# The start, the seam and the end of a two-layer block on one core: first loads in order of use, the last recurrence chunk in two, quarter stores

## The chip, the cores and the metric

The kernel runs on one core of a Trainium2 chip, which has eight. The metric is the device time of one execution in microseconds. TensorE (PE) multiplies, VectorE (DVE), ScalarE (ACT) and GpSimd (POOL) compute on tiles, and the sync engine's queue (SP) issues every DMA. All data is float32; each matmul therefore shows as two PE passes in the trace.

## The reference, cut to what matters

For x of shape (2, 4096, 256), with `ln` a layer norm without weights and `shift` a step by one position:

```
h = ln(x);  r, k, v = (h*mix_j + shift(h)*(1 - mix_j)) @ W_j.T          # j = r, k, v
wkv = scan over 4096 positions of (k, v) with a decay per channel, kept in log space
x1  = x + group_norm(sigmoid(r) * wkv) @ W_o.T      # statistics over all positions of a batch, per head
y   = ln(x1)
two layers:  y += local_attention(shift_token(y))    # 8 heads of 64, window 128, rotary
             y += gated_mlp(ln(shift_token(y)))      # 256 -> 2*682 -> 256, gelu
out = x1 + y
```

`shift_token` moves only the second half of the channels by one position. The group norm needs the whole sequence of a batch, so attention of a batch can't begin before its recurrence has ended.

## The kernel before

**Order.** The code does not issue instructions as it is written. `Plan` records every operation with its engine, its tiles and a row number (`plan.at`), and at the end `order` places them: each engine takes the operation that can start first by a table of costs, and among those the one with the lowest row and number. The result is one fixed queue per engine. In the trace nearly all instructions therefore have the line of `give` (L497, or L491 and L493 for `scaled`, which may go to DVE or ACT).

**Recurrence of batch 0.** `Recurrence(0, T, ...)` works through 4096 positions in eight chunks of T = 512. `ahead(c)` loads x, normalises it (`normed`), transposes it to xT (channels on partitions) and projects it to k, v, r. The mixing is folded into the weights: wnow is the weight times mix, wold the weight times (1 - mix), so each output takes four products (two halves of the channels, present and previous position). `scans(c)` does three scans on DVE for each half of the channels (m, the log sum, aa), exponentials and logarithms on ACT, and puts q to DRAM (zd) with its statistics; after the last chunk `group_norm` makes scale and offset (gmv, dm, group). Chunk c+1 is projected while chunk c is scanned. Part of this batch's tiles are lent from buffers that attention uses later (x, h, hm, hT, sq, t, qk); the rest lie in `arena`.

**Recurrence of batch 1** runs in chunks of TR = 256 beside the attention of batch 0, over the first 54 rows. It mixes x on DVE (`change`, `mix_x`) and uses the plain weights, which are loaded into wold again.

**Attention and MLP.** A row n is 128 positions of one layer and batch; a block k is four rows (512 positions). There are 128 rows and 32 blocks. A block's x is x plus the group-normed z times W_o (`mixed_out`, wot), or layer one's result from xmd. In each row there are the projection of the next row, scores, softmax, the values of the last row and the output projection (wo); `shift` copies x to h by DMA, h is normalised, and after four rows `transpose_h`, `gate`, `value` and `down` do the MLP (w, hm). `store` writes the block: to xmd for layer one; for layer two it loads x1, adds it on POOL and writes 512 KB to the output.

**Start.** SP loads mats, vec, mask, lnp, b1, qks, then wold (768 KB), then the first two chunks of x (512 KB each), then the weights of attention and MLP. The twelve scalings of the weights are the first large operations in DVE's queue:

```
for j in (1, 2, 0):
    for i in range(2):
        for dst, t in ((self.wnow, vec[:, j, i : i + 1]), (wold, omt[:, j, i : i + 1])):
            nc.vector.tensor_scalar(dst[:, j, i, :], wold[:, j, i, :], t, None, ALU.mult)
```

Of the kernel before, what the change touches and what calls it, by code (L numbers as in the profile page):

```python
# [15 lines left out]
P = 128  # L16
# [17 lines left out]
R_SLOTS = 54  # L34

FIRST = (
    ("xT", 2 * T + 2, 2),
    ("m ls aa", 2 * T + 2, 1),
    ("wnow", 6 * D, 1),
    ("k v r x f g e q", 2 * T, 2),  # L40
)
SECOND = (
    ("xT", 2 * TR + 2, 2),
    ("m ls aa", 2 * TR + 2, 1),
    ("x k v r", 2 * TR, 2),
    ("d f g e q", 2 * TR, 1),
    ("xm", 2 * TR, 3),
)
RA = 10764
VFIRST = True  # L50
# [122 lines left out]
class Plan:  # L173


    def __init__(self, nc, sbuf, psum, dram):
        self.nc, self.sbuf, self.psum, self.dram_pool = nc, sbuf, psum, dram
        for e in ("tensor", "vector", "scalar", "gpsimd", "sync", "either"):
            setattr(self, e, Engine(self, e))
        self.places, self.turns = {}, {}  # L180
        self.pieces, self.open, self.row = [], None, 0.0
        self.kept = 0
# [46 lines left out]
    def note(self, eng, name, args, kw):  # L229
# [35 lines left out]
        for v in ins:  # L265
            first = v.place.first
            if v.place.psum and first is not None and eng != "tensor":
                first.deps.update(d for d in before if d.n < first.n and d not in v.place.users)
# [232 lines left out]
def kernel(ctx: ExitStack, tc: tile.TileContext, a: dict, out: bass.AP):  # L501
# [12 lines left out]
    nc.sync.dma_start(out=mats, in_=a["c_mats"])  # L514
# [30 lines left out]
    nc.sync.dma_start(out=vec, in_=a["p_rwkv"])  # L545
    wot = tile_of([P, 2, D], "wot")

    wdec = tile_of([P, 2], "wdec")
    nc.scalar.activation(wdec, vec[:, 3, :], AF.Exp)
    nc.vector.tensor_scalar(wdec, wdec, -1.0, None, ALU.mult)  # L550

    mwu = tile_of([P, 2], "mwu")
    nc.vector.tensor_tensor(mwu, wdec, vec[:, 4, :], ALU.add)
    nc.vector.tensor_scalar(mwu, mwu, -0.5, None, ALU.mult)
# [5 lines left out]
    wold = tile_of([P, 3, 2, D], "wold")  # L560

    class Recurrence:


        def __init__(self, b, tr, spots, mixed):
            self.b, self.tr, self.mixed, self.spots = b, tr, mixed, spots
            self.turns = {}
            self.n = S // tr


            nc.sync.dma_start(out=wold, in_=a["w_rkv"])
            if not mixed:
                self.wnow = plan.view(*self.spot("wnow"), [P, 3, 2, D])
                omt = tile_of([P, 3, 2], "omt")
                nc.vector.tensor_scalar(omt, vec[:, 0:3, :], -1.0, 1.0, ALU.mult, ALU.add)
                for j in (1, 2, 0):
                    for i in range(2):
                        for dst, t in ((self.wnow, vec[:, j, i : i + 1]), (wold, omt[:, j, i : i + 1])):
                            nc.vector.tensor_scalar(dst[:, j, i, :], wold[:, j, i, :], t, None, ALU.mult)
            self.stats = tile_of([P, 2, S // 256, 6], "stats")[:, :, : self.n, :]  # L580

            self.m, self.ls, self.aa = (
                plan.view(*self.spot(t), [P, 2, tr + 1]) for t in ("m", "ls", "aa")
            )
            self.s0 = tile_of([P, 2], "s0")
# [3 lines left out]
            self.chunks = [{} for _ in range(self.n)]  # L589
# [6 lines left out]
        def t(self, tag, cols=None):  # L596
            return plan.view(*self.spot(tag), [P, 2, cols or self.tr])


        def load(self, c):  # L600
            x = self.chunks[c]["x"] = plan.view(*self.spot("x"), [P, self.tr // P, D])
            nc.sync.dma_start(
                out=x,
                in_=a["x"][self.b, c * self.tr : (c + 1) * self.tr, :].rearrange(
                    "(w p) d -> p w d", p=P
                ),
            )

        def normed(self, c):
            nw = self.tr // P  # L610
            x = self.chunks[c]["x"]
            mv = tile_of([P, NW, 2], "r_mv", 2)
            for w in range(nw):
                st = tile_of([P, 6], "r_st", 4)
                nc.vector.bn_stats(st, x[:, w, :])
                nc.vector.bn_aggr(mv[:, w, :], st)
            rs = tile_of([P, NW], "r_rs", 2)
            rsqrt_of(rs[:, :nw], mv[:, :nw, 1], nw, LN_EPS, ALU.add)
            nb = tile_of([P, NW], "r_nb", 2)
            nc.vector.scalar_tensor_tensor(  # L620
                nb[:, :nw], mv[:, :nw, 0], -1.0, rs[:, :nw], ALU.mult, ALU.mult
            )
            for w in range(nw):
                nc.scalar.activation(
                    x[:, w, :], x[:, w, :], AF.Identity, bias=nb[:, w : w + 1], scale=rs[:, w : w + 1]
                )

        def transposed(self, c):
            x, tr = self.chunks[c]["x"], self.tr
# [4 lines left out]
            else:  # L634
                nc.gpsimd.tensor_copy(xT[:, :, 0:1], self.chunks[c - 1]["xT"][:, :, tr : tr + 1])
# [10 lines left out]
        def change(self, c):  # L646
            ch = self.chunks[c]
            d = ch["d"] = self.t("d")
            nc.vector.tensor_tensor(d, ch["xT"][:, :, 1:], ch["xT"][:, :, : self.tr], ALU.subtract)

        def mix_x(self, c, j):
            ch = self.chunks[c]
            xm = ch["xm", j] = self.t("xm")
            for i in range(2):
# [4 lines left out]
                    ch["xT"][:, i, : self.tr],  # L659
                    ALU.mult,  # L660
                    ALU.add,
                )

        def project(self, c, j):

            ch, tr = self.chunks[c], self.tr
            if self.mixed:
                self.mix_x(c, j)
                parts = [(wold, ch["xm", j][:, i, :], i) for i in range(2)]
            else:  # L670
                parts = [
                    (wt, ch["xT"][:, i, off : off + tr], i)
                    for i in range(2)
                    for wt, off in ((self.wnow, 1), (wold, 0))
                ]
            dst = ch[j] = self.t("rkv"[j])
# [19 lines left out]
        def ahead(self, c):  # L696
# [3 lines left out]
            if self.mixed:  # L700
                self.change(c)
            for j in (1, 2, 0):
                self.project(c, j)


        def factors(self, y, c):

            g, e = self.t("g"), self.t("e")
# [6 lines left out]
        def scans(self, c):  # L715
            ch, tr = self.chunks[c], self.tr
# [3 lines left out]
            if c:  # L720
                nc.gpsimd.tensor_copy(m[:, :, 0:1], m[:, :, tr : tr + 1])
                nc.gpsimd.tensor_copy(ls[:, :, 0:1], ls[:, :, tr : tr + 1])
                nc.gpsimd.tensor_copy(aa[:, :, 0:1], aa[:, :, tr : tr + 1])
            f = self.t("f")
            for h in range(2):
                wd = wdec[:, h : h + 1]
                nc.vector.tensor_tensor_scan(
                    m[:, h, 1:], wd.to_broadcast([P, tr]), k[:, h, :], m[:, h, 0:1], ALU.add, ALU.max
# [10 lines left out]
            nc.scalar.activation(ls[:, :, 1:], e, AF.Ln)  # L739
# [7 lines left out]
            for h in range(2):  # L747
                nc.vector.tensor_tensor_scan(
                    aa[:, h, 1:], g[:, h, :], e[:, h, :], aa[:, h, 0:1], ALU.mult, ALU.add
                )  # L750
            q = self.t("q")
            for hs in hs2:
# [5 lines left out]
                for h in range(hs.start, hs.stop):  # L758
                    nc.vector.bn_stats(self.stats[:, h, c, :], q[:, h, :])
# [659 lines left out]
```

## Time and profile before

| | us |
|---|---|
| Median of 3 runs (range) | 3133.59 (3133.59 to 3134.77) |
| The profiled execution's own time | 3134.43 |
| Its span, first to last instruction | 3132.6 |
| PE / DVE / ACT / POOL busy | 3054.1 / 2528.4 / 1834.6 / 1323.1 |
| Mean granted clock of PE | 0.993 |
| DMA moved | 131.78 MB, 42 GB/s on average |

Busy time counts an engine as busy from an instruction's start to its end; the ends of matmuls are modelled. In a stage where PE is busy all the time, only less PE work could shorten it; where it stands idle, what it waits for sets the time. Times in the profile are microseconds from the first instruction.

### The profile page before, as it was taken

How to read it: one execution, taken by the hardware profiler on the slowest of the kernel's cores; microseconds unless marked ns; L12 is line 12 of the kernel's file. 1: busy time of each engine (PE TensorE's matmuls, PEld its weight loads, DVE VectorE, ACT ScalarE, POOL GpSimd, SP SyncE). 2: the span in 40 equal slices, each digit the busy share in tenths (PEclk: the TensorE clock that was granted, in tenths of full speed). 3: DMA queues.
4: the chain of work that ended last, by engine and by line, in shares of the span. 5: the costliest groups of instructions: out<-in, count | busy, mean ns of one | idle time of the engine just before them, and what ended most of it. 6: DMA issues, size and time to landing. Idle time of an engine off the chain costs nothing.

```text
span 3132.6 us, 47494 instructions
## 1 busy us (share of the span) xinstructions
PE 3054.1 (97%) x16296; PEld 2016.0 (64%) x16296; DVE 2528.4 (81%) x6287; ACT 1834.6 (59%) x4355; POOL 1323.1 (42%) x1544
## 2 busy tenths in 40 slices
PE   7969999999999999999999999999999999999998
PEld 3436666666666666666666666666666666666665
DVE  6979998888888988887778787777877877777774
ACT  5767766666666667655545555544555555555552
POOL 1217544445444444444444444444434443444431
PEclk9989999999999999999999999999999999999999
DMA  3122001111111111111112111111001111111000
GB/s 128 43 75 71 31 31 42 34 33 43 47 32 58 39 38 42 37 35 35 33 32 69 62 44 38 41 39 40 33 26 48 39 35 35 34 31 34 28 22 25
DMA packets 106386, 131.78 MB, mean 42 GB/s; under 512 B 11680, under 2 KB 89760, under 8 KB 105632
## 3 DMA queue, kind: packets, MB, share of 16 engines
q1 hardware_dynamic: 106144, 128.75, 13.1%
q8 instruction: 128, 2.10, 0.3%
q14 instruction: 114, 0.93, 0.1%
HBM read 78.38 MB, written 33.55 MB: 36 GB/s over the span
## 4 chain that ended last, share of the span: by engine, by line
PE 81%; DVE 9%; ACT 4%; issue 2%; DMA 1%; POOL 1%; SPq 0%; POOLq 0%; DVEq 0%; ACTq 0%
PE bank L497 81%; DVE arena L497 3%; DVE sq L497 1%; ACT arena L497 1%; DMA h<-x 1%; DVE qk L497 1%; ACT pr L497 1%; ACT L497 1%; DVE pr L497 1%; DVE pT L497 1%; DVE x L497 0%; DVE hm L497 0%; POOL rs L497 0%; ACT qk L497 0%; DVE pr L491 0%
## 5 line engine op out<-in xcount | busy, mean ns | idle before, releaser
L497 PE MATMUL bank<-wqkv,xT 128*128 128x512 f32 x1536 | 732.4, 600 | 0.0
L497 ACT ACTIVATE pr<-pr,nmx 128x256 f32<-128x256 f32 (+1 forms) x1024 | 504.6, 494 | 385.5 <-DVE nmx L497 385.3
L497 POOL TENSOR_TENSOR t<-qk,tab 128x256 f32<-128x256 f32 x512 | 385.9, 774 | 692.2 <-DVE qk L497 355.6
L497 PE MATMUL bank<-hT,w 128*128 128x512 f32 (+1 forms) x1408 | 645.7, 593 | 0.2 <-ACT hT L497 0.2
L497 PEld LDWEIGHTS bank<-hT,w 128*128 128x128 f32 (+1 forms) x1408 | 254.2, 189 | 254.6 <-issue 248.2
L497 PEld LDWEIGHTS bank<-wqkv,xT 128*128 128x128 f32 x1536 | 264.2, 190 | 228.4 <-issue 226.1
L497 DVE CUSTOM_DVE_ANT_0 pr<-bank,mask 128x256 f32<-128x256 f32 (+1 forms) x1024 | 373.3, 414 | 40.2 <-PE bank L497 40.0
L497 POOL TENSOR_TENSOR rn<-rn,mhalf 128x16 f32<-128x16 f32 x128 | 376.9, 2945 | 10.4
L497 PE MATMUL bank<-w,hm 128*128 128x256 f32 x1536 | 352.4, 379 | 1.8 <-DVE hm L497 1.8
L497 PEld LDWEIGHTS bank<-w,hm 128*128 128x128 f32 x1536 | 288.9, 190 | 59.8 <-issue 21.5
L497 PEld LDWEIGHTS bank<-mats,pr 128*128 128x128 f32 x2016 | 237.1, 141 | 117.0 <-issue 76.3
L493 ACT ACTIVATE pr<-pr,sums 128x256 f32<-128x256 f32 (+1 forms) x615 | 285.9, 496 | 44.1 <-DVE sums L497 43.0
L497 PEld LDWEIGHTS bank<-pT,vt 128*64 128x64 f32 x4032 | 217.5, 137 | 93.8 <-issue 85.4
L497 PE MATMUL bank<-mats,pr 128*128 128x128 f32 x2016 | 270.7, 273 | 6.3 <-DVE pr L491 4.3
L497 PE MATMUL bank<-kT,qT 64*128 64x256 f32 (+1 forms) x2048 | 253.7, 386 | 3.3 <-DVE nmx L497 3.3
L497 PE MATMUL bank<-pT,vt 128*64 128x128 f32 x4032 | 248.4, 276 | 0.0
L497 PE MATMUL bank<-wo,oT 128*128 128x256 f32 x1024 | 244.8, 382 | 0.7 <-ACT oT L497 0.7
L497 POOL TENSOR_TENSOR tab<-tab,qks 128x256 f32<-128x256 f32 x128 | 164.5, 1286 | 187.6 <-DMA tab<-in_c_rot_dram 159.3
L497 PEld LDWEIGHTS bank<-wo,oT 128*128 128x128 f32 x1024 | 192.2, 190 | 76.9 <-issue 36.4
L497 ACT COPY pT<-bank 128x512 f32<-128x512 f32 (+1 forms) x280 | 153.0, 573 | 123.9 <-PE bank L497 123.0
L497 DVE TENSOR_TENSOR x<-x,bank 128x256 f32<-128x256 f32 (+1 forms) x288 | 128.0, 445 | 119.5 <-PE bank L497 115.5
L497 PEld LDWEIGHTS bank<-kT,qT 64*128 64x128 f32 x2048 | 184.8, 186 | 44.2 <-issue 20.7
(140 smaller groups left out, 4893.8 us busy)
## 6 DMA issues: line engine op xcount, KB each, us to landing
tab<-in_c_rot_dram SPq DMA_DIRECT2D x128, 128.0 KB
x<-in_x_dram SPq DMA_DIRECT2D x20, 512.0 KB
z<-zd SPq DMA_DIRECT2D x16, 512.0 KB
x1d<-x SPq DMA_DIRECT2D x16, 512.0 KB
x<-x1d SPq DMA_DIRECT2D x16, 512.0 KB
h<-x SPq DMA_DIRECT2D x128, 64.0 KB
xmd<-x SPq DMA_DIRECT2D x16, 512.0 KB
x<-xmd SPq DMA_DIRECT2D x16, 512.0 KB
```

Of the source, the lines that this page charges most:

```text
L493: self.nc.scalar.activation(dst, src, AF.Copy, scale=scale)
L497: getattr(getattr(self.nc, o.eng), name)(*args, **kw)
```

## The change

- **Loads.** Batch 0's first chunk of x comes first, in four pieces of 128 positions; then mats, vec and wold in three parts (k, v, r). `normed` works on two pieces at a time. wot, mask, lnp, b1 and qks are loaded after the first chunk's scans (`plan.hold` makes a load wait for an operation), the weights of attention and MLP after those of chunks 1 to 3.
- **Weight scaling** goes to DVE or ACT, in the order k, v, r, and is placed behind the first chunk's normalisation.
- **The last chunk** of batch 0 is two chunks of 256. Batch 1's first chunk is projected behind it with the scaled weights (`split`); only then is wold loaded again and the rest of batch 1 mixed on DVE (`mixed`).
- **Other places.** `ahead` puts load, normalisation and transposition one row earlier; z is scaled on ACT instead of POOL; `transpose_qk` is recorded earlier in its row; the first row of the next block's h is copied at the end of the block before it.
- **x1** is loaded at a layer-two block's first `shift`, and added on POOL row by row two rows later, before `down` adds the MLP. `store` is gone: `down` stores each quarter of a block (128 KB).
- **early**: in the last block an MLP value's bank need not wait for the other inputs of the operation that reads it.

The diff, cut to its core:

```diff
+AHEAD = 1
-            if v.place.psum and first is not None and eng != "tensor":
-                first.deps.update(d for d in before if d.n < first.n and d not in v.place.users)
+            if v.place.psum and first is not None and eng != "tensor" and not self.early:
+                first.deps.update(d for d in before if d.n < first.n)
+        if self.hold is not None:
+            before.add(self.hold)
...
         def load(self, c):
+            nw = self.len[c] // P
+            x = self.chunks[c]["x"] = plan.view(*self.spot("x"), [P, nw, D])
+            step = 1 if c == 0 else nw
+            for w in range(0, nw, step):
+                o = self.off[c] + w * P
+                nc.sync.dma_start(
+                    out=x[:, w : w + step, :],
+                    in_=a["x"][self.b, o : o + step * P, :].rearrange("(w p) d -> p w d", p=P),
+                )
...
+        def mixed(self, c, j):
+            ch, tr = self.chunks[c], self.len[c]
+            if "d" not in ch:
+                d = ch["d"] = self.t("d", tr)
+                nc.vector.tensor_tensor(d, ch["xT"][:, :, 1:], ch["xT"][:, :, :tr], ALU.subtract)
+            xm = self.t("xm", tr)
+            for i in range(2):
+                nc.vector.scalar_tensor_tensor(
+                    xm[:, i, :], ch["d"][:, i, :], vec[:, j, i : i + 1],
+                    ch["xT"][:, i, :tr], ALU.mult, ALU.add,
+                )
+            return [(wraw, xm[:, i, :], i) for i in range(2)]
+
+        def split(self, c, j):
+            ch, tr = self.chunks[c], self.len[c]
+            return [
+                (wt, ch["xT"][:, i, off : off + tr], i)
+                for i in range(2)
+                for wt, off in ((wnow, 1), (wold, 0))
+            ]
...
+        def ahead(self, c, how):
+            row = plan.row
+            plan.at(row - 1)
             self.load(c)
             self.normed(c)
             self.transposed(c)
+            plan.at(row)
             for j in (1, 2, 0):
+                self.project(c, j, how)
...
         for h in range(2):
-            nc.gpsimd.tensor_scalar(
-                z[:, h, :], z[:, h, :], g[:, 0, h : h + 1], g[:, 1, h : h + 1], ALU.mult, ALU.add
+            nc.scalar.activation(
+                z[:, h, :], z[:, h, :], AF.Identity, bias=g[:, 1, h : h + 1], scale=g[:, 0, h : h + 1]
             )
...
+        elif c < NB - 1:
+            hs[k + 1] = tile_of([P, NW, D], "h", 2)
+            nc.sync.dma_start(out=hs[k + 1][0:1, 0, P:], in_=x[P - 1 : P, w, P:])
         nc.sync.dma_start(out=h[:, w, :P], in_=x[:, w, :P])
+        if l:
+            if w == 0:
+                x1s[k] = tile_of([P, NW, D], "x1")
+                nc.sync.dma_start(out=x1s[k], in_=x1d[b][c])
+            row = plan.row
+            plan.at(row + 2)
+            nc.gpsimd.tensor_tensor(x[:, w, :], x[:, w, :], x1s[k][:, w, :], ALU.add)
+            plan.at(row)
...
         nc.vector.tensor_tensor(x, x, py, ALU.add)
-
-    def store(k):
         l, b, c = blocks[k]
-        x = xs.pop(k)
-        if l == 0:
-            nc.sync.dma_start(out=xmd[b][c], in_=x)
-            return
-        x1 = tile_of([P, NW, D], "x1")
-        nc.sync.dma_start(out=x1, in_=x1d[b][c])
-        nc.gpsimd.tensor_tensor(x, x, x1, ALU.add)
-        nc.sync.dma_start(
-            out=out[b, c * T : (c + 1) * T, :].rearrange("(w p) d -> p w d", p=P), in_=x
-        )
+        o = c * T + w * P
+        to = out[b, o : o + P, :] if l else xmd[b][c][:, w, :]
+        nc.sync.dma_start(out=to, in_=x)
...
-    rec = Recurrence(0, T, spots(FIRST, lent), False)
-    rec.ahead(0)
+    plan.at(-101)
+    rec = Recurrence(0, [T] * (NB - 1) + [T // 2] * 2, T, spots[0])
+    rec.start()
+    rec.load(0)
+    nc.sync.dma_start(out=mats, in_=a["c_mats"])
+    nc.sync.dma_start(out=vec, in_=a["p_rwkv"])
+    for j in (1, 2, 0):
+        nc.sync.dma_start(out=wold[:, j], in_=a["w_rkv"][:, j])
+    rec.normed(0)
+    small_vectors()
+
+    for j in (1, 2, 0):
+        for i in range(2):
+            for dst, t in ((wnow, vec[:, j, i : i + 1]), (wold, omt[:, j, i : i + 1])):
+                nc.either.scaled(dst[:, j, i, :], wold[:, j, i, :], t)
+    rec.transposed(0)
+    for j in (1, 2, 0):
+        rec.project(0, j, rec.split)
+    rec2 = Recurrence(1, [TR] * (S // TR), TR, spots[1])
     for c in range(rec.n):
         if c + 1 < rec.n:
             plan.at(-90 + c)
-            rec.ahead(c + 1)
-        if c == 0:
-            nc.sync.dma_start(out=wot, in_=a["w_ot"])
-        if c == 1:
-            weights(0, "qkvo12")
+            rec.ahead(c + 1, rec.split)
         plan.at(-90 + c)
         rec.scans(c)
+        plan.hold = plan.pieces[-1][0]
+        if c == 0:
+            later_loads()
+        if 0 < c < 4:
+            weights(0, ("qkv", "o", "12")[c - 1])
+        plan.hold = None
     rec.group_norm()
+    for c in range(AHEAD):
+        plan.at(-0.5)
+        rec2.ahead(c, rec2.split)
+    plan.at(-0.5)
+    nc.sync.dma_start(out=wraw, in_=a["w_rkv"])
+    rec2.start()
```

## The prediction

> **What bounds the kernel now.** I read the page's first two parts, then busy time by stage, then the order of time where TensorE (PE) is not busy.
>
> ```profile
> PE 3054.1 (97%) x16296; PEld 2016.0 (64%) x16296; DVE 2528.4 (81%) x6287; ACT 1834.6 (59%) x4355; POOL 1323.1 (42%) x1544
> ```
>
> PE bounds: 3132.6 - 3054.1 = 78.5 us is all it stands still. The busy time by stage (start:end, length, PE, PEld, DVE, ACT, POOL, granted clock, DMA share, GB/s) says where:
>
> ```profile
> 0.00:20.00 20.00, 2.23 (x7) 1.35 (x8) 7.67 (x34) 3.56 (x6) 3.19 (x16) 1.00 0.86 295
> ...
> 40.00:200.00 160.00, 154.36 (x398) 70.08 (x396) 140.31 (x223) 122.36 (x208) 37.41 (x51) 1.00 0.14 50
> 200.00:240.00 40.00, 18.46 (x69) 15.04 (x70) 29.57 (x75) 15.82 (x26) 11.57 (x24) 0.66 0.34 112
> 240.00:360.00 120.00, 106.54 (x610) 73.06 (x609) 109.46 (x289) 84.76 (x203) 80.53 (x99) 0.96 0.17 55
> 360.00:600.00 240.00, 236.90 (x1278) 156.95 (x1277) 214.38 (x534) 164.07 (x379) 103.12 (x130) 1.00 0.09 29
> 600.00:1500.00 900.00, 894.70 (x4948) 608.18 (x4947) 778.94 (x1934) 569.98 (x1350) 405.98 (x461) 1.00 0.13 40
> 1500.00:3080.00 1580.00, 1580.00 (x8792) 1056.18 (x8792) 1224.37 (x3166) 855.59 (x2161) 675.08 (x757) 1.00 0.12 38
> ```
>
> Idle: 17.8 at the start, 5.6 in the first recurrence, 21.5 between recurrence and attention (there the clock is 0.66 too), 13.5 while attention fills, 3.1 and 5.3 until 1500, none to 3080, 11.7 at the end. From 1500 on a change can only cost. The places, in order of time (start, length, engine, instruction, idle before it):
>
> ```profile
> 10.48 0.62 DVE L497 TENSOR_SCALAR arena<-wold,vec 128x256 f32<-128x256 f32 x2 [6.64 <-DMA wold<-in_w_rkv_dram]
> ...
> 17.72 2.80 PE L497 MATMUL bank<-mats,hm 128*128 128x128 f32 x8 [17.72 <-ACT hm L497]
> ...
> 20.46 1.95 PE L497 MATMUL bank<-arena 128*128 128x512 f32 x2
> ...
> 219.36 0.59 PE L497 MATMUL bank<-gmv,mats 128*128 128x2 f32 x2 [20.01 <-DVE gmv L497]
> ...
> 231.25 1.02 PE L497 MATMUL bank<-wot,z 128*128 128x256 f32 x4
> ...
> 3126.29 2.34 POOL L497 TENSOR_TENSOR x<-x,x 128x1024 f32<-128x1024 f32 x1 [33.02 <-DVE x L497]
> 3128.65 0.39 SPq L497 DMA_DIRECT2D out_dram<-x  x1
> ```
>
> The normalisation of the first x stands on VectorE (DVE) behind twelve weight scalings that wait for one 768 KB load. In the middle PE has run out of projections at 199.35 and waits for the last chunk's scans to give the group statistics (gmv). At the end a POOL addition stands between the last matmul and the store.
>
> **Part A, the start: -9.9.** After the change SP issues four 128 KB pieces of x first, then mats, vec and wold in three pieces, at 0.4 to 0.5 us each. Before, vec was issued at 1.17 and had landed at 3.04 (1.9 us), and 1.37 MB had landed by 10.48, about 175 GB/s once it flowed. So x pieces land at about 3.3 to 5, mats and vec before 6, wold's k third near 7.5. Statistics of two pieces to nb: 0.4 + 0.16 on DVE and 1.1 on POOL, as at 219.50 to 220.83 before. ScalarE (ACT) then has two x pieces (0.52 each), wdec, one weight scaling that waits for wold's k, and the last two x pieces: done near 9.3. Transposes and two copies of 0.6: projection runs from 11.0. Before, 48 passes of 0.43 ended at 41.56, so it effectively ran from 20.9. Bounds: 8 if the k third lands at 9.5, 11.5 if loads flow at the 405 GB/s seen between 10 and 20 us. The clock is taken as full, as the first row shows (1.00 while PE idles).
>
> **Part B, the middle: -6.4 more, to the first wot matmul.** Everything up to the last recurrence chunk shifts by A: PE needs 22.5 us a chunk, DVE some 19.7, both nearly full, so no more than the shift. The last 512 columns become two chunks of 256 with the same columns in all (48 matmuls of 256 for 24 of 512), ending near 189.4. Behind them the other batch's first chunk is projected with 24 matmuls of 256 where 12 did (wnow and wold instead of mixed x): 12 x 2 x 0.215 = +5.2 us of PE work, put where PE idled; six mixing operations of 0.42 and a subtraction go from DVE (-3.1). PE is through at about 200.5.
>
> Then DVE decides. Counting the changed order from the first half chunk's m scan to gmv, with start-to-start times of before: 14 scans of 256 columns x 0.66, 2 of 512 x 1.2, 7 operations of 256 x 0.42, 25 of 512 elements x 0.60, 14 statistics x 0.31, 11 tiny ones 1.1: 34.9 us. That includes the other batch's normalisation, copies and mixing, which are ahead of gmv in DVE's queue. It starts where chunk 7's scan stood, 183.28 - 9.9 = 173.4; with 4 us of waits (6.6 before) gmv comes near 212, not 219.36. A rule speaks against the halves: each chunk needs ACT's table changed to Ln and back, two changes more. The row:
>
> ```profile
> 201.90 1.28 ACT L497 ACT_TABLE_LOAD   x1 [1.40 <-DVE qk L497]
> 203.19 1.06 ACT L497 ACTIVATE arena<-qk 128x1024 f32<-128x1024 f32 x1
> ```
>
> It costs 1.28, and Ln starts 1.29 after it. The Trainium skill ("ScalarE: Activation LUTs", What ACT_TABLE_LOAD costs) charges a drain of about 1.38 besides, 2.66 in all. By the row the two cost 2.6, part of it under the other half's DVE work, and are inside my 4 us; by the page 5.3, and gmv would come near 214.5. I take the row.
>
> From gmv to the first wot matmul: before 11.9, behind 16 projection passes at half clock; after, 1.4 to dm, 4.8 to group as before, then z on ACT (2 x 0.55) instead of POOL: 7.4, so 219.4. The reload of wold is issued only when the last half chunk frees x buffers (near 208) behind two 512 KB loads of x; 1.79 MB at about 260 GB/s (the rate between 200 and 204 before): landed near 216, and the 8 passes ahead of wot hide it. So wot comes 11.9 us earlier, with 8 projection matmuls (3.4) and 8 transposes (1.1) more already done: 16.3 in all, A included.
>
> Clock: before, it was 0.50 from 204 to 230:
>
> ```profile
> 204.00:219.00 15.00, 0.00 (x0) 0.00 (x0) 12.03 (x21) 7.13 (x12) 0.00 (x0) 0.50 0.32 107
> 219.00:230.00 11.00, 8.46 (x24) 6.30 (x25) 8.98 (x33) 3.28 (x6) 7.05 (x12) 0.50 0.22 72
> ```
>
> The skill ("TensorE: Matmul & The Clock Gate", Part 1) has it halve after one idle window of about 3.4 us. By it a remaining gap of 11 us goes cold again, so I give nothing back for the clock; only a gap under 3.4 would save about 4 more. The same rule makes idle the cold default, which the start's 1.00 contradicts; by it A would shrink only if the warm-up cost differed between the two kernels.
>
> **Part C, attention's beginning (240 to 600): -3.** DVE is 91% busy there. It loses 3.1 of mixing, POOL loses 32 z operations (25.9 us), ACT gains 32 x 0.59 at 70% busy. In the only long stall PE held h transposes for a normalised h for 4.3 us; the changed order has all eight of the block after the next row's wo, about half a row later. What other stalls the new order makes the trace cannot say: from -8 to +6, and I take -3, near DVE's saving.
>
> **Part D, the end: -0.9.** x1 is added four times per block by POOL two rows ahead, so after the last DVE addition (3126.20) a 128 KB store follows. Before: 2.43 to the issue, 3.95 to the span's end with 512 KB. With 128 KB I estimate 2.8: -3.5 in all (bounds -2.4 with equal landing, -4). Against it: before, the last wo was followed by 12 down passes (2.6 us) which hid part of the wait for the last h; in the changed order these come ahead of wo and PE goes straight to h: +2.6. The early flag gives nothing, since PE runs without a gap from 3094.97 to 3125.7.
>
> **Nothing for the rest.** Stores in quarters are 96 issues more of 0.4 us on SP, which has four or five a row of 21.3 us; later loads and the moved 0.5 KB row of h likewise; x1's load waits on POOL's last addition to the one buffer, with h copies queued behind it on SP. The cover is the distance from h to its transposes: shift at 2668.24, h transposed at 2688.89, some 10 us after it is ready. Without this cover each of 16 blocks would cost its lateness. I keep -1 to +4.
>
> **Sum.** -16.3 - 3 - 0.9 = -20.2 against the profiled execution's 3134.43 gives 3114.2. That execution lies 0.84 above the median of 3133.59, inside its spread of 1.2; I predict 3114.
>
> **The rivals.** (1) Only the start moves: half chunks meet the same chain DVE-ACT-table, ACT with two more tables and the other batch's four normalisations is late, gmv near 217, or attention's beginning eats the lead: 3121 to 3126. For it: DVE and ACT both near full before gmv. Against: half-chunk work interleaves. Chance 0.15. (2) The gap nearly closes: waits vanish, gmv by 206, PE stays warm: 6 + 4 more, 3101 to 3107. Chance 0.15. (3) Slower: SP's queue. In 16 layer-two blocks the x1 load waits for POOL's last addition and holds the next row's h copies; the price is the lateness beyond the 10 us of cover, and it decides from 1.3 us per block (16 x 1.3 = 21), so an x1 load 11 us late. POOL is 42% busy, which speaks against. 3136 to 3150, chance 0.03. (4) The lead is real but waited away: 3127 to 3140, 0.04. Forecast 0.63, its own range 3107 to 3121.
>
> Range 3102 to 3126: bounds of A (+-1.8), gmv (+-4), C (-5, +9), D (+-1). What a measurement can tell from no change is about 0.2%, 6.3 us; below 3127.3 is faster: 0.93, same 0.04, slower 0.03.
>
> **What would show it.** First transposes near 8 and projection from 11; gmv near 212 with PE idle 10 us before it, clock 0.5 again; wot near 219; last h stall of about 7 us; span end 3 us after the last DVE addition; 1500 to 3080 still full. Projection from later than 14, gmv after 217, or PE gaps between 600 and 3080 make it wrong.

## The result, and the profile after

The changed kernel takes 3111.93 us (median of 6 runs, 3107.07 to 3113.52) where the kernel before takes 3134.47 beside it (3133.59 to 3136.11): a ratio of 0.9926, 95% interval 0.9913 to 0.9939, or 22.5 us. The prediction was 3114.0, range 3102 to 3126. The profiled execution took 3112.78, in the upper half of its runs, with a span of 3110.8.

The page's busy time of the changed kernel:

```profile
PE 3061.6 (98%) x16368; PEld 2030.8 (65%) x16368; DVE 2539.1 (82%) x6306; ACT 1865.0 (60%) x4401; POOL 1339.6 (43%) x1581
```

PE now stands still for 3110.8 - 3061.6 = 49.2 us instead of 78.5, and works 7.5 us more, of which 5.2 are the twelve additional matmuls of 256. So 29.3 us of idle time went. Busy time by stage says where (start:end, length, PE, PEld, DVE, ACT, POOL, clock, DMA share, GB/s):

```profile
0.00:20.00 20.00, 12.52 (x26) 5.79 (x27) 9.42 (x31) 7.04 (x14) 4.70 (x20) 1.00 0.47 145
...
40.00:200.00 160.00, 148.98 (x427) 77.23 (x425) 135.84 (x245) 124.93 (x211) 45.66 (x67) 0.99 0.22 76
200.00:240.00 40.00, 32.09 (x118) 25.63 (x119) 31.82 (x75) 24.41 (x40) 11.26 (x22) 0.76 0.40 132
240.00:360.00 120.00, 118.58 (x695) 79.91 (x694) 114.31 (x323) 93.53 (x228) 84.78 (x101) 1.00 0.16 51
360.00:600.00 240.00, 238.09 (x1301) 161.27 (x1300) 216.55 (x543) 165.77 (x385) 108.45 (x133) 1.00 0.12 37
600.00:1500.00 900.00, 892.86 (x4925) 603.06 (x4924) 774.11 (x1904) 581.42 (x1362) 403.34 (x462) 1.00 0.13 39
```

At the start, 7.5 us idle in the first 20 instead of 17.8. Between 40 and 240, 18.9 instead of 27.2: the one gap of 20 us is broken up, not closed. Between 240 and 360, 1.4 instead of 13.5: here the most was won. Between 600 and 1500, 7.1 instead of 5.3: a small loss. PE in order of time (idle before it in brackets):

```profile
10.17 2.08 PE L497 MATMUL bank<-arena 128*128 128x512 f32 x2
12.04 1.91 PE L497 MATMUL bank<-arena,wold 128*128 128x512 f32 x2
...
35.60 1.13 PE L497 MATMUL bank<-arena 128*128 128x512 f32 x2 [1.59 <-DVE arena L497]
...
200.15 1.40 PE L497 MATMUL bank<-mats,arena 128*128 128x128 f32 x4 [6.51 <-ACT arena L497]
...
218.58 0.38 PE L497 MATMUL bank<-gmv,mats 128*128 128x2 f32 x2 [3.63 <-DVE gmv L497]
...
227.19 6.50 PE L497 MATMUL bank<-wot,z 128*128 128x256 f32 x16 [2.21 <-ACT z L497]
...
3075.40 1.33 PE L497 MATMUL bank<-mats,h 128*128 128x128 f32 x5 [7.51 <-DVE h L497]
```

gmv comes at 218.58, only 0.8 before its old place (219.36), and wot at 227.19 instead of 231.25. The 6.5 us at 200 are new. ACT in order of time shows what they wait for:

```profile
190.82 1.28 ACT L497 ACT_TABLE_LOAD   x1
...
193.80 1.28 ACT L497 ACT_TABLE_LOAD   x1
...
199.50 2.06 ACT L497 ACTIVATE arena<-arena,r_nb,r_rs 128x256 f32<-128x256 f32 x4
```

The other batch's first chunk is normalised (199.50) behind two table loads and the exponentials of a half chunk. At the end the last store follows DVE's last addition directly:

```profile
3107.67 0.42 DVE L497 TENSOR_TENSOR x<-x,bank 128x256 f32<-128x256 f32 x1 [2.17 <-PE bank L497]
3108.12 0.33 SPq L497 DMA_DIRECT2D out_dram<-x  x1
```

Two marks serve below: the start of row 0's scores and of row 5's. Idle time of PE up to the first, between the two, and the half-clock windows up to 600 in the trace's clock records, which begin with the first change to full clock:

| kernel | idle to row 0 | idle rows 0 to 5 | half clock | median |
|---|---|---|---|---|
| before | 46.9 | 11.5 | 37.5 | 3134.5 |
| changed | 28.4 | 0.0 | 23.9 | 3111.9 |
| 1: last chunk whole | 28.5 | 8.8 | 27.3 | 3121.6 |
| 2: first chunk not ahead | 38.4 | 1.0 | 23.9 | 3113.9 |
| 3: z on POOL | 33.7 | 8.4 | 37.5 | 3131.7 |
| 5: before, z on ACT | 45.7 | 9.6 | 34.1 | 3127.8 |
| 9: whole old start | 38.8 | 0.0 | 27.3 | 3123.4 |

Five parts of the change were undone, each by itself, in the changed kernel, and a few things were added. The earlier place of `transpose_qk`, the early copy of h's first row, `early` and the quarter stores of layer one alone were not undone singly. The kernel before, run beside them, had medians of 3134.3 to 3135.2. One caution: run 8 has the changed kernel's order up to the last row, and yet its profile is 3 us ahead from row 0 on, with 20.5 us of half clock instead of 23.9. Both wait 2.04 us for the second half chunk's transposed x, the changed kernel at 181.34 and run 8 at 180.62; behind it the changed kernel has half clock from 181.65 to 185.06, and run 8 has none. Differences of 3 us between two profiles' early parts are therefore no finding by themselves.

### The profile page after: what moved, and what is told of

The parts are those of the page before. It is cut to its first block, busy times and chain, and to the rows that moved or that the text cites. A ratio compares the mean times of both kernels' runs of the same rounds, so it can differ in the third digit from the quotient of the medians.

```text
span 3110.8 us, 47943 instructions
## 1 busy us (share of the span) xinstructions
PE 3061.6 (98%) x16368; PEld 2030.8 (65%) x16368; DVE 2539.1 (82%) x6306; ACT 1865.0 (60%) x4401; POOL 1339.6 (43%) x1581
## 3 DMA queue, kind: packets, MB, share of 16 engines
q1 hardware_dynamic: 114592, 128.75, 13.2%
## 4 chain that ended last, share of the span: by engine, by line
PE 80%; DVE 10%; ACT 4%; POOL 2%; issue 2%; DMA 2%; SPq 0%; POOLq 0%; DVEq 0%; ACTq 0%
PE bank L497 80%; DVE arena L497 3%; ACT arena L497 1%; DMA h<-x 1%; DVE pr L497 1%; DVE sq L497 1%; DVE qk L497 1%; POOL rs L497 1%; ACT L497 1%; DVE hm L497 1%; POOL rn L497 1%; DVE x L497 1%; ACT qk L497 0%; SPq L497 0%; DVE pT L497 0%
## 5 line engine op out<-in xcount | busy, mean ns | idle before, releaser
L497 POOL TENSOR_TENSOR rn<-rn,mhalf 128x16 f32<-128x16 f32 x128 | 380.9, 2976 | 10.3
L497 PEld LDWEIGHTS bank<-kT,qT 64*128 64x128 f32 x2048 | 184.9, 186 | 44.6 <-issue 19.8
L497 POOL TENSOR_SCALAR rs<-mv 128x1 f32<-128x1 f32 x192 | 98.4, 517 | 248.4 <-DVE mv L497 242.2
L497 PE MATMUL bank<-arena,wold 128*128 128x256 f32 (+1 forms) x600 | 193.1, 447 | 0.0
```

The source lines that it names most:

```text
L497: getattr(getattr(self.nc, o.eng), name)(*args, **kw)
```

## The experiments

**1. The last chunk whole.**

```diff
-    rec = Recurrence(0, [T] * (NB - 1) + [T // 2] * 2, T, spots[0])
+    rec = Recurrence(0, [T] * NB, T, spots[0])
```

> Changed kernel with the last recurrence chunk of batch 0 whole (512 columns) again; the rest stays, the other batch's first chunk behind it too. Theory (the halves cost more than they bring: two more table changes and a ping-pong between ACT and DVE; the start alone would have brought gmv to about 219.4 - 8.5 = 211): gmv near 213 to 216 instead of 218.6, time 2 to 5 us below the changed kernel (3107 to 3110). Rival (the halves shorten the last chain, as the prediction had it): gmv near 222, time 3 to 6 us above it (3115 to 3118).

3121.63 us (3120.78 to 3122.18), ratio 0.9958 (0.9943 to 0.9973): 9.7 above. Both theories missed. PE in order of time:

```profile
211.08 0.58 PE L497 MATMUL bank<-gmv,mats 128*128 128x2 f32 x2 [9.62 <-DVE gmv L497]
...
218.01 5.37 PE L497 MATMUL bank<-wot,z 128*128 128x256 f32 x16 [4.11 <-ACT z L497]
```

gmv is 7.5 us earlier without the halves and wot 9.2, as my theory said, and still the kernel is slower. What PE waited for between row 0 and row 5 (total, times, longest), and the busy time there:

```profile
PE bank L497 <- DVE h L497: 4.2, 1, 4.2
PE bank L497 <- DVE pr L491: 1.7, 1, 1.7
PE bank L497 <- DVE qk L497: 1.5, 1, 1.5
```

```profile
251.50:339.70 88.20, 79.38 (x497) 56.22 (x496) 80.94 (x217) 64.73 (x165) 53.82 (x63) 0.94 0.14 46
```

The same stretch of the changed kernel:

```profile
262.10:333.90 71.80, 71.80 (x481) 51.86 (x480) 69.11 (x202) 54.93 (x152) 57.15 (x61) 1.00 0.15 49
```

With the whole chunk attention begins 10.6 us earlier, but with 10.7 us less matmul work done ahead, and DVE has 80.9 us to do in five rows instead of 69.1. PE waits for it 8.8 us, and partly at half clock. Up to row 0 both idle alike (28.5 and 28.4). The halves pay in rows 0 to 5, not at gmv: at row 5 this kernel is 5.8 us behind. Another 3.5 us come after row 5, and their cause is open.

**2. The other batch's first chunk in row 0, mixed.**

```diff
-AHEAD = 1
+AHEAD = 0
...
+                if c == 0:
+                    rec2.ahead(0, rec2.mixed)
```

> Changed kernel with the other batch's first chunk in row 0 again (mixed x, 12 matmuls of 256 instead of 24), not ahead of attention. Theory (the projection ahead fills only what the gap had free; the lead in attention's beginning comes with it): PE work 5.2 us less, gap in front of gmv about 8 us longer but gmv 2 to 4 us earlier, stalls between 240 and 360 back by 3 to 6 us: 1 to 5 us above the changed kernel. Rival (stalls in attention's beginning have another cause, z on POOL or order): idle time between 240 and 360 stays near 1.4 us, time 3 us below the changed kernel to equal.

3113.87 us (3112.85 to 3115.74), ratio 0.9934 (0.9919 to 0.9949): 1.9 above, inside both intervals. Ten more us idle up to row 0, gmv at 213.65, 4.9 earlier, 11.1 us less matmul time spent when row 5 is reached, at the same time (333.9 in both). Only 5.2 us of it are the additional matmuls; the rest isn't made up later either (PE is busy for 3050.4 us in all, where the changed kernel has 3061.6), as the changed kernel projects partly at half clock. The theory holds in size and in gmv's direction, though only 1 us of the stalls came back. The additional matmuls were paid for by the gap, and little more.

**3. z on POOL again.**

```diff
-            nc.scalar.activation(
-                z[:, h, :], z[:, h, :], AF.Identity, bias=g[:, 1, h : h + 1], scale=g[:, 0, h : h + 1]
-            )
+            nc.gpsimd.tensor_scalar(
+                z[:, h, :], z[:, h, :], g[:, 0, h : h + 1], g[:, 1, h : h + 1], ALU.mult, ALU.add
+            )
```

> Changed kernel with z scaled on POOL again instead of ACT. Theory (z on ACT is a small part: first wot about 1.5 us earlier, the rest is the lead): 1 to 3 us above the changed kernel, idle time between 240 and 360 below 5 us. Rival (POOL's 32 z operations of 0.8 us held up h and so made the stalls of attention's beginning): idle time between 240 and 360 back at 8 to 13 us, time 6 to 12 us above.

3131.73 us (median of 20, 3130.0 to 3134.47), ratio 0.9992 (0.9985 to 0.9999): 19.8 above, nearly the kernel before. The theory fell, the rival is right and still too small. Busy time of the stage:

```profile
240.00:360.00 120.00, 108.12 (x595) 73.58 (x594) 101.92 (x279) 78.19 (x187) 82.54 (x101) 0.93 0.16 52
```

11.9 us idle instead of 1.4. POOL in order of time:

```profile
260.10 0.72 POOL L497 TENSOR_TENSOR t<-qk,tab 128x256 f32<-128x256 f32 x1
260.81 4.12 POOL L497 TENSOR_SCALAR z<-z,group 128x512 f32<-128x512 f32 x2
...
265.42 3.26 POOL L497 TENSOR_TENSOR t<-qk,tab 128x256 f32<-128x256 f32 x4
```

The operations on z by their shortest, median and longest time (ns):

```profile
L497 POOL TENSOR_SCALAR z<-z,group x32: 758/768/3365, 225.0 to 2150.1; 128x512 f32<-128x512 f32 x32
...
  PE bank L497: 7.7, 3
```

The last line is PE's waiting for z itself: 7.7 us in three waits before row 0's scores. And what PE waits for then:

```profile
282.40 1.97 PE L497 MATMUL bank<-mats,qk 128*128 128x128 f32 x8 [2.15 <-DVE qk L497]
```

Two z operations stand in the middle of the first rows' rotations, and take 4.1 us where two take 1.5 elsewhere. During them DVE runs two-input additions and products (261.51 to 264.46). The Trainium skill ("SBUF — State Buffer", SBUF: two separate sides) says that such a DVE operation and a POOL operation exclude each other for their whole length; the 3365 against the median of 768 fits that. It is one operation; of the other 31 only one takes longer than 0.81 us (1.92, at 238.37). PE waits for z, for 2.2 us in the changed kernel and for 7.7 here. qk comes late too, PE waits 5.1 us for qk and 3.2 for pr in rows 0 to 5, and falls back to half clock (37.5 us in all instead of 23.9). Idle 63.6 us instead of 49.2 and busy 3067.0 instead of 3061.6 make the 20. How they divide among the stretched operation, the place of z in POOL's queue and the other order that comes with it, these runs do not show.

**4. The other batch's first chunk normalised earlier.**

```diff
-        plan.at(-0.5)
-        rec2.ahead(c, rec2.split)
+        plan.at(-83.5)
+        rec2.load(c)
+        rec2.normed(c)
+        plan.at(-82.5)
+        rec2.transposed(c)
+        plan.at(-0.5)
+        for j in (1, 2, 0):
+            rec2.project(c, j, rec2.split)
```

> Changed kernel with one thing moved: the other batch's first chunk is normalised and transposed ahead of the last half chunk's exponentials in ACT's queue (a planning row of -83.5 instead of -1.5). Theory (that normalisation standing behind two table changes made PE wait 6.5 us at 200 and go cold): that wait falls under 3 us, the cold window there goes, time 3 to 5 us below the changed kernel. Rival (DVE's chain to gmv decides; what PE gains it waits for at gmv): gmv within 1 us of 218.6, time within 2 us of the changed kernel.

3110.97 us (3109.44 to 3112.0), ratio 0.9924 (0.9909 to 0.9939): the rival. PE in order of time:

```profile
211.94 1.40 PE L497 MATMUL bank<-mats,arena 128*128 128x128 f32 x4 [6.47 <-ACT arena L497]
...
228.37 5.63 PE L497 MATMUL bank<-wot,z 128*128 128x256 f32 x16 [3.38 <-ACT z L497]
```

The wait at 200 is gone and stands at 212, for the next chunk's normalisation. gmv comes at 218.72; DVE had it ready at 217.92, only 0.6 earlier than in the changed kernel. The chain over ACT and DVE sets it.

**5. z on ACT alone, in the kernel before.** The edit of run 3 turned round, in the kernel before.

> The kernel before with one part of the change alone: z scaled on ACT instead of POOL. Theory (z on POOL stands in the middle of row 0's rotations and makes qk late, and this alone costs some 10 to 20 us in whatever kernel): 8 to 15 us below the kernel before (3119 to 3126), idle time between 240 and 360 falls from 13.5 to below 5. Rival (it costs that much only where the other batch's first chunk is ahead of it and POOL has more to do then; in the order of before z was not in the way): within 5 us of the kernel before.

3127.84 us (3126.93 to 3129.06), ratio 0.9979 (0.9969 to 0.9988): 6.7 faster, between the two. Idle time between 240 and 360 is 10.4, not below 5, and the gap in front of gmv stays at 20.0 us. Alone, this part brings a third of what its removal costs in run 3: rows 0 to 5 still stall for 9.6 us, about as in run 1, which lacks the halves too. Of the 5.8 us between the two profiles 2.0 are won at row 5 and the others by row 30; what wins those is open.

**6. The start's order of before.**

```diff
-    rec.load(0)
     nc.sync.dma_start(out=mats, in_=a["c_mats"])
     nc.sync.dma_start(out=vec, in_=a["p_rwkv"])
-    for j in (1, 2, 0):
-        nc.sync.dma_start(out=wold[:, j], in_=a["w_rkv"][:, j])
-    rec.normed(0)
+    nc.sync.dma_start(out=wold, in_=a["w_rkv"])
+    rec.load(0)
...
+    rec.normed(0)
     rec.transposed(0)
...
-            step = 1 if c == 0 else nw
+            step = nw
```

The scalings are on DVE too.

> Changed kernel with the start of before: mats, vec, wold in one load and x in one load behind them, all twelve scalings on DVE ahead of the normalisation. Theory (the start is worth its 8.6 us by the effective start of projection, and nothing later gives it back): 7 to 10 us above the changed kernel, effective start of projection near 21. Rival (the gap in front of gmv takes part of it up, since ACT and not the start sets it): 2 to 5 us above.

3112.1 us (3111.04 to 3113.07), ratio 0.9929 (0.9915 to 0.9942): no difference. Only half of the old start came back, since the other constants and weights still stood behind: wold had landed at 6.17, not at 10.48. PE in order of time:

```profile
38.09 1.91 PE L497 MATMUL bank<-mats,arena 128*128 128x128 f32 x16
```

That is chunk 1's transposes, 5.1 us behind the changed kernel (32.97). By chunk 6 it is 0.2 behind (146.04 to 145.86). The order transposes two chunks at once here, PE does not wait for transposed x at the chunks' boundaries, and a chunk takes 21.6 us instead of 22.6. The waits, 1.59 at 35.60 and 0.3 to 0.9 at the next four boundaries, were 4.2 us in the changed kernel.

**7. Warming matmuls at the start.**

```diff
+    plan.at(-102)
+    wt = plan.view(plan.places["hm_0"], 0, [P, P])
+    nc.gpsimd.memset(wt, 0.0)
+    pw = bank([P, T])
+    for _ in range(12):
+        nc.tensor.matmul(pw[:, :P], wt, wt, start=True, stop=True)
+    plan.at(-101)
```

> Changed kernel with twelve matmuls of 128 columns on a zeroed tile added on PE in the first 6 us; their result is used by nothing. Theory (PE is at half clock until 14.5 although the profile's clock column shows 1.00 there, because it is idle until 6.1): the first projection passes are 0.43 apart instead of 0.85, the record of full clock comes before 10, projection ends 2 us earlier, time 1.5 to 2.5 us below the changed kernel. Rival (the spacing of the first passes comes from the transfers or from weights that come late, not from the clock): passes still 0.85 apart until 14.5, time the same.

3110.23 us (3108.97 to 3110.72), ratio 0.9923 (0.991 to 0.9935): 1.7 below in the median, not beyond the intervals. The mechanism is plain in PE's order of time:

```profile
0.98 4.31 PE L497 MATMUL bank<-hm 128*128 128x128 f32 x24 [0.98 <-POOL hm L497]
...
9.69 1.13 PE L497 MATMUL bank<-arena 128*128 128x512 f32 x2 [0.34 <-DVE arena L497]
10.66 1.02 PE L497 MATMUL bank<-arena,wold 128*128 128x512 f32 x2
```

Two passes start 0.85 to 0.97 after the two before; in the changed kernel it is 1.87 and 1.71 (10.17, 12.04, 13.75). The clock records have full speed from 3.9 instead of 14.4, and chunk 1's transposes start at 30.41 instead of 32.97.

**8. One down pass held behind the last wo.**

```diff
         if behind:
             output(n - 1)
+            wo_done = plan.pieces[-2][-1]
...
-        fill(n, 2)
+        fill(n, 2, wo_done if n == NN else None)
```

The third pass of the second last block then depends on `wo_done`.

> Changed kernel with one block of six matmuls (the last down of the second last block) held until the last wo is done, so that it stands in the wait for the last h. Theory (the end pays 2.6 us for having all down passes ahead of wo): wait for h falls from 7.5 to near 4.9, time 2 to 2.7 us below the changed kernel. Rival (the pass ahead of wo covers the copy of oT, so that wo then waits as long): time the same.

3111.28 us (3108.29 to 3111.35), ratio 0.9923 (0.991 to 0.9935): not told apart by the time. PE in order of time:

```profile
3060.95 1.99 PE L497 MATMUL bank<-wo,oT 128*128 128x256 f32 x8 [0.79 <-DVE oT L497]
...
3070.77 1.33 PE L497 MATMUL bank<-mats,h 128*128 128x128 f32 x5 [4.91 <-DVE h L497]
```

The wait for h falls by 2.6 to 4.91; 0.79 of it returns at oT. Measured from row 120, the span ends 1.7 us earlier.

**9. The whole old start.** Run 6's edit, and the other loads back in front:

```diff
     nc.sync.dma_start(out=vec, in_=a["p_rwkv"])
+    later_loads()
     nc.sync.dma_start(out=wold, in_=a["w_rkv"])
...
-        plan.hold = plan.pieces[-1][0]
-        if c == 0:
-            later_loads()
-        if 0 < c < 4:
-            weights(0, ("qkv", "o", "12")[c - 1])
-        plan.hold = None
+        if c == 1:
+            weights(0, "qkvo12")
```

> Changed kernel with the whole start of before, the other constants and the weights of layer one in front of and beside wold as well (run 6 had left those late, and there wold's load had landed at 6.2 instead of 10.5). Theory (the start moves the time only by what the recurrence passes on; run 6 started its projection 5 us late and had caught up by the sixth chunk, because PE then does not wait for transposed x at the chunks' boundaries, 4.2 us in the changed kernel): projection effectively from 20 to 21, half or less of the 8.6 us left at the first wot, 2 to 5 us above the changed kernel. Rival (run 6 was a lucky order, and the start passes through whole): 7 to 10 us above.

3123.39 us (3120.23 to 3125.56), ratio 0.9964 (0.9951 to 0.9976): 11.5 above, more than the rival had. My theory fell. PE's first work:

```profile
17.35 2.94 PE L497 MATMUL bank<-mats,arena 128*128 128x128 f32 x8 [17.35 <-ACT arena L497]
```

Chunk 1's transposes come at 43.28, 10.3 behind, and rows 0 to 127 stay 11.2 to 11.6 behind. At its end the start has passed through whole, though not evenly: chunk 6's transposes are 8.3 behind, and a wait of 3.7 us for chunk 8's transposed x brings the rest back. The kernel before itself has chunk 1's transposes at 41.98, 1.3 earlier than here, with full clock recorded from 22.15 instead of 25.0; so the 11.5 are rather more than the old start's own cost. Run 6 was a start 5 us late with an order that caught up; what that order alone is worth is another matter (run 11).

**10. Matmuls that fill the waits.** Runs 7 and 8 together, and

```diff
+    plan.hold = last8
+    plan.at(-0.25)
+    for _ in range(24):
+        pw = bank([P, T])
+        nc.tensor.matmul(pw[:, :P], ident, ident, start=True, stop=True)
+    plan.hold = None
```

with 14 more in front of gmv.

> A better version: the changed kernel with the twelve warming matmuls of run 7, the held down pass of run 8, and besides 24 and 14 matmuls of 128 columns on the identity, used by nothing, that the order puts into the two waits of PE in front of the other batch's first chunk and of gmv. Theory (work after these waits runs at half clock, 24 us of cold windows in all, some 7 to 9 us of work at half speed): cold windows between 180 and 235 fall under 10 us, time 6 to 9 us below the changed kernel (3103 to 3106). Rival (the clock there does not set the end, since DVE and ACT decide when gmv and z come): only the 3 to 4 us of runs 7 and 8 (3107 to 3109).

3111.74 us (3109.32 to 3116.12), ratio 0.9928 (0.9913 to 0.9943): the rival, and not even the gain of runs 7 and 8. PE in order of time:

```profile
189.18 5.52 PE L497 MATMUL bank<-mats 128*128 128x128 f32 x48
...
214.28 0.38 PE L497 MATMUL bank<-gmv,mats 128*128 128x2 f32 x2 [0.54 <-DVE gmv L497]
...
222.89 5.28 PE L497 MATMUL bank<-wot,z 128*128 128x256 f32 x16 [3.98 <-ACT z L497]
```

Half clock before 600 falls to 6.8 us, but gmv (214.28) and wot (222.89) come only 0.3 before run 7's (214.62, 223.23). The wait for z is longer instead, and 3.5 us of stalls come back in rows 0 to 5, where the fillers also changed the order.

**11. The same, and the chunks' transposes half a row earlier** (`plan.at(row - 1.5)` for `plan.at(row - 1)` in `ahead`, for the first batch).

> As the run before, and the loading, normalising and transposing of the first batch's next chunks put half a planning row earlier (-1.5 instead of -1), so that copies of transposed x come ahead of the scans of the chunk before. Theory (PE waits 4.2 us in all for those copies at the chunks' boundaries): these waits fall under 1.5 us and the time falls by 2 to 3 us more than without it. Rival (the scans that now come later set the end of the recurrence): gmv not earlier, time the same or 1 to 3 us above the run before.

3108.88 us (3107.85 to 3109.61), ratio 0.9917 (0.9902 to 0.9932): 2.9 below run 10 in the median, intervals overlapping. Chunks 1 to 5 follow each other by 21.7 us as in run 6, the next takes 24.9, and PE was cold again from 7.7 to 14.5. Against run 10's profile row 0 is 0.8 earlier and row 50 is 1.5. The theory has the sign; much of the gain is given back at the following chunk.

**12. The old end of each block.** The addition of x1 and the store as in the kernel before:

```diff
-        to = out[b, o : o + P, :] if l else xmd[b][c][:, w, :]
-        nc.sync.dma_start(out=to, in_=x)
...
+        nc.sync.dma_start(out=x1, in_=x1d[b][c])
+        nc.gpsimd.tensor_tensor(x, x, x1, ALU.add)
+        nc.sync.dma_start(
+            out=out[b, c * T : (c + 1) * T, :].rearrange("(w p) d -> p w d", p=P), in_=x
+        )
```

> Changed kernel with the old end of each block: x1 loaded and added on POOL for the whole block after the last down pass, and one store of 512 KB. Theory (the prediction's 3.5 us): last output ends 3 to 4 us later after DVE's last addition (6.2 to 6.5 instead of 2.7), time 3 to 4 us above the changed kernel. Rival (x1 loads and additions two rows ahead hold something up inside the blocks): stalls in layer two vanish with the old end and the time is the same or lower.

3107.19 us (3106.66 to 3107.88), ratio 0.9912 (0.9897 to 0.9927): 4.7 below the changed kernel in the median, intervals overlapping. Both theories are half right. The end, POOL and SP in order of time:

```profile
3098.66 2.34 POOL L497 TENSOR_TENSOR x<-x,x 128x1024 f32<-128x1024 f32 x1 [33.89 <-DVE x L497]
3101.03 0.39 SPq L497 DMA_DIRECT2D out_dram<-x  x1
```

From DVE's last addition (its end, 3098.58) to the span's end (3104.9) it is 6.3 us, in the changed kernel 2.7: 3.6, as expected. But in layer two, while the other batch's recurrence still runs, the new end makes PE wait. Busy time between 1000 and 1400 of this run:

```profile
1000.00:1400.00 400.00, 399.58 (x2227) 269.80 (x2225) 348.81 (x841) 261.63 (x606) 174.36 (x192) 1.00 0.12 37
```

of the changed kernel:

```profile
1000.00:1400.00 400.00, 395.86 (x2173) 265.56 (x2172) 346.40 (x826) 262.93 (x609) 184.73 (x201) 1.00 0.12 38
```

and of the kernel before:

```profile
1000.00:1400.00 400.00, 397.92 (x2180) 269.15 (x2179) 350.63 (x845) 258.13 (x608) 176.23 (x191) 1.00 0.13 41
```

Idle 0.4, 4.1 and 2.1 us; POOL works 10.4 us less with the old end. From row 30 to row 50 this kernel takes 460.7 us, the changed kernel and the ten other runs that have the new end 465.1 to 466.1, the kernel before 463.7: the old end gains 5.2 us there and keeps them. Up to 999 us its queues are those of the changed kernel, so the 2.3 us by which its profile leads at row 30 are not the edit's. Whether it is the 17 smaller additions on POOL (0.73 us each, where the old end has 3 large ones) or the order that comes with them is open.

## Why the prediction was right, and where not

The sum was -20.2 and the profiled execution is 21.7 faster, but three terms were off and paid for each other: parts A and B were sized too large, part C too small. That the sum came out so near is in part luck, and gmv after 217, one of the prediction's own signs of being wrong, did happen.

- **Part A, -9.9.** Measured -9.0: chunk 0's projection ends at 32.97 instead of 41.98. (41.56 is where its last pass starts; with its end the working gives -10.3.) wold's first third and nb came as worked out, and projection began at 10.17. The step that failed is "the clock is taken as full": the 48 passes took 22.8 us where 20.6 were counted, and in the kernel before 21.5, so 1.3 of the lead went. (In the seven profiles with this start the lead lies between 8.8 and 10.8, by the moment at which full clock comes.) I read the column's 1.00 while PE idles as a granted clock and held it against the Trainium skill's rule ("TensorE: Matmul & The Clock Gate", Part 1: idle means half clock until a sustained busy stretch). It is the absence of a record (the first one of the kernel before is at 22.15): the passes from 12.04 on stand 0.85 apart, and run 7, which warms PE, has them at 0.43. The page was right. The lead did pass through, but that the first half chunk's m scan started at 173.44 where I had 173.4 is in part luck: PE's lead was 9.0 us at chunk 1 and 8.0 at chunk 6 (145.86 for 153.85), and chunk 7's projection no longer waits for its transposed x (1.55 before).
- **Part B, wot 11.9 earlier.** Measured 4.1. Chunk 8's projections ended at 193.6 instead of 189.4, with PE's smaller lead, the wait at 181.34 and the half clock behind it, and gmv came at 218.6 instead of 212. The failed step is "34.9 us of work with 4 us of waits" on DVE (its items add to 35.0): between 173.44 and 218.50 it was busy 36.84 and idle 8.2. What ended its longer waits (total, times, longest):

```profile
DVE x L497 <- ACT arena L497: 2.5, 2, 2.2
DVE qk L497 <- ACT qk L497: 2.1, 2, 1.9
DVE arena L497 <- PE bank L497: 2.1, 1, 2.1
DVE r_nb L497 <- POOL r_rs L497: 1.1, 2, 0.8
```

4.6 us are ACT's, and the 2.1 of PE's projection follow its wait at 200 for ACT's normalisation. This is rival 1's mechanism, ACT late with two more tables and the other batch's normalisation, at 218.6 for its 217; run 4 shows that taking one of these waits away moves it on. The table row held: Ln starts 1.29 after its load, with no drain behind. Much of parts A and B together, -16.3, came as work done ahead: row 0's scores start only 1.9 us earlier, but PE has worked 233.65 us by then where it had worked 217.1. Without the additional 5.2 us that makes a lead of about 13.2, as an estimate (it leaves out what ran at half clock).
- **Part C, -3.** Idle time between 240 and 600 fell by 13.2, and half clock there vanished. Of the 21.8 us between the spans about 8.6 are left for what comes from row 0 on, more than the -8 that I had as the most. The failed step is the size "near DVE's saving" of 3.1, with POOL's 32 z operations listed without a price. By run 3 that was the dearest edit of all in this kernel, 19.8 us: PE waited 5.5 us longer for z itself, and 8.3 us for qk and pr in rows 0 to 5. By run 1 the halves count here too.
- **Part D, -0.9.** The end behaves as worked out: 2.7 us from the last addition to the span's end (3 predicted), a wait of 7.5 us for the last h (7 predicted). From row 120 to the span's end the changed kernel takes 212.9 us and the kernel before 213.4, a gain of 0.5 for the 0.9 worked out; run 12, the old end in the changed order, takes 214.5.
- **Nothing for the rest, -1 to +4.** Idle time between 600 and 1500 rose by 1.8, inside the range, but by run 12 the new end costs 3.7 us of idle time between 1000 and 1400. The failed step is that only SP's queue was asked about: the cover that I named, the distance from h to its transposes, belongs to it. What became late are other inputs, while the second recurrence shares DVE and POOL: of the 4.1 us PE waits 1.4 for qk, 1.3 for oT and 1.3 for pr.
- **The rivals.** Rival 1's mechanism happened and its time did not, since part C was much larger. Rival 2's gap did not close. Rival 3, SP's queue, did not show: PE is without a gap from 1500 to 3060. Nor was the lead waited away, as rival 4 had it.

Undone one by one the parts cost 11.5 (start), 9.7 (halves), 1.9 (projection ahead), 19.8 (z) and -4.7 (the end), 38.2 in all against 22.5. They are not additive: either z on POOL or the whole chunk alone brings 8 to 9 us of stalls back in rows 0 to 5, and only both together take the kernel before's 11.5 away. The fastest of all kernels here is run 12; it was not run with the start's warming matmuls.

## What to carry to other kernels

Price a moved operation on the engine that it leaves, by what stood behind it in that engine's queue, and not only by the busy time that it takes along: 32 operations of 0.77 us taken off POOL were worth 19.8 us in one kernel and 6.7 in another. A wait taken away in front of a chain over two other engines comes back as the next wait (runs 4 and 10); what counts is idle time up to a mark well behind the chain, and whether the stage after it has stalls. Undo the parts of a bundle singly: one of five here, the new end, seems to be a loss hidden by the others (its medians' intervals overlap, its stage in layer two is slower in every profile).

## What the runs showed of the hardware

- PE starts at half clock: passes of 512 columns stand 0.85 us apart at first and 0.43 later. In the seven profiles with the changed kernel's start full speed is recorded from between 11.4 and 14.6, after first transposes at 6.1 with gaps between them, and chunk 1's transposes start between 31.2 and 33.2 accordingly. With unbroken work from 0.98 it is recorded from 3.9 (run 7).
- The same wait of 2.04 us in front of the second half chunk's projection was followed by half clock in the changed kernel and runs 3 and 4, and not in runs 2, 7, 8 and 12.
- A POOL operation of 0.77 us took up to 3.4 while DVE ran operations with two inputs.
- Two executions with the same order of instructions up to the last row lay 3 us apart from row 0 on, with 23.9 and 20.5 us of half clock.
